# Two stacked graph-attention layers on one core: another written order, score tiles of 32x64, bias rows on VectorE, b2 in norm 1's shift, norm 3 on ScalarE

## The chip, the cores and the metric

The kernel runs on one core of one Trainium2 chip. The metric is the device time of that core in microseconds; three runs of the kernel before gave 3072.71, 3078.34 and 3072.94, so the median is 3072.94. Each profile is one further execution. An engine's records in it are written PE (TensorE's matmuls), PEld (its weight loads), DVE (VectorE), ACT (ScalarE), POOL (GpSimd) and SP (SyncE, which here only issues DMAs).

## The reference

32 independent graphs of 512 nodes with 256 features in f32, and an integer adjacency matrix of 512x512 for each. Two layers, both with a residual and a final layer norm; all norms are over the 256 features. Attention has 8 heads of 32.

```python
# layer 0, with allowed = (adj > 0) | (adj.T > 0) | eye
q, k, v = split(x @ Wqkv.T + bqkv)                      # per head
attn = softmax(where(allowed, (q / sqrt(32)) @ k.T, -inf)) @ v
x1 = layernorm(x + attn @ Wo.T + bo) * g1 + be1          # norm 1
y = relu(x1 @ W1.T + b1) @ W2.T + b2                     # hidden size 1024
z = layernorm(x1 + y) * g2 + be2                         # norm 2
x2 = layernorm(x + z)                                    # norm 3
# layer 1, with the mask adj != 0
q, k, v = x2 @ Wq.T + bq, x2 @ Wk.T + bk, x2 @ Wv.T + bv
attn = softmax(where(adj != 0, q @ k.T / sqrt(32), -inf)) @ v
out = layernorm(x2 + attn @ Wo.T + bo)                   # norm 4
```

## The kernel before

**Tiling.** A graph's 512 nodes are NQ = 4 blocks of 128; its 256 features are ND = 2 blocks of 128, each with HPC = 4 heads. Scores are computed transposed, with keys on partitions: score step k (0 to 7) is four heads of one feature block against one block of 128 keys, so p[k] is a tile of 128 x (4 heads x 512 queries). Per layer there are eight such steps. Each is: `scores` (four matmuls psS into four PSUM banks, L342, and Exp on ScalarE, L346), `masked` (a multiplication by the 0/1 mask on VectorE, L351), `product` (four matmuls psA = v.T p, accumulated over the four key blocks, L359; after the fourth, a copy to cT on ScalarE, L369). Row sums of p come from tiles of p that are first added up, partly by accumulating DMAs on GpSimd's queue (`pair`, L374), partly on VectorE (`fold`, L378), and then multiplied by a matrix of ones (`sums`, psR, L399). `divide` (L411 to L418) transposes the sums in blocks of 32, inverts, transposes back and scales cT; two small GpSimd adds (L414, L415) collect a guard against overflow, which selects a slow general path after the main program when it trips (it doesn't here).

**Dense parts.** `query_key` (psQK), `value` (psV), `project` (psO), `hidden` (psH) and `mlp` (psF) all go through `dense` (L171): with `wide=True` one matmul of 128x128 weights, otherwise four of 128x32, one for each quarter of the output partitions. `transpose` (psT, L308) turns x1 and x2 by matmuls with the identity, always 128x128. psS uses tiles of 32x128: contraction over the 32 features of a head, 128 keys. The tensors are f32 throughout, and an f32 matmul stands in the trace as two records.

**Norms.** y = PSUM + residual (L446), bn_stats and bn_aggr (L427, L428), 1/sqrt(var + eps) on GpSimd in two instructions (`root`, L433 and L434), then for norms 1 and 2 two VectorE instructions (L441, L442) with g and b, for norm 3 one VectorE instruction (`norm3`, L507), for norm 4 a small VectorE instruction (`offset`, L516: -mean/std) and an ACTIVATE with scale and bias on ScalarE (`norm4`, L521).

**Bias rows.** bov[layer] = bv Wo + bo is computed once (`value_bias`, L163, L166). Four accumulating DMAs per graph on GpSimd's queue (`add_row`, L174) add rows to a whole 128 x (4 x 256) tile: bov[0] to x1 (which starts as a second load of x), be2 to x, b2 to x1 after `transpose`, and bov[1] to x2.

**Input.** `cast` (L209) has GpSimd's queue turn adj into bf16 in HBM; `entries` loads it straight and, by four DMA transposes, transposed, and `masks` (L227 to L231) makes the two masks from them. x reaches its transposed form xT without TensorE: a DMA transpose of 16-bit halves (`flip`, L266), four small DMAs that sort the halves (`sort`, L283), and two ScalarE copies (`join`, L296); only graph 0 uses `transpose`.

**Order.** Nothing is scheduled automatically. The calls stand one under another by hand in `opening`, `period` and `closing`, inside `tc.manual_schedule()`, and each engine and each DMA queue runs its instructions strictly in that order, waiting where data or a buffer is not there. A period holds 70 groups of TensorE work, one graph's worth, but from several graphs (a, b, c, d, e, oldest first) at different stages: here layer 1's end of a, layer 0's end and layer 1 of b, layer 0 of c, the input of d and e. Buffers that set a limit: one psS tile (four banks, so the next scores wait for the Exp before), one accumulator psA, three banks of tag "d" for all other PSUM results, eight p tiles.

Of the kernel before, what the change touches and what calls it, by code (L numbers as in the profile page):

```python
# [18 lines left out]
EPS = 1e-5  # L19
# [8 lines left out]
def kernel(ctx: ExitStack, tc: tile.TileContext, t: dict, out: bass.AP):  # L28
# [88 lines left out]
    bo.append(spread("L1_gnn_bo"))  # L117

# [31 lines left out]
    def plain(pools: ExitStack):  # L150
# [6 lines left out]
        BEATS = ND * NQ  # L157
# [9 lines left out]

        def dense(out, lhsT, rhs, start, stop, wide):

            for at in (slice(0, P),) if wide else [slice(j * HD, (j + 1) * HD) for j in range(HPC)]:  # L170
                nc.tensor.matmul(out[at], lhsT[:, at], rhs, start=start, stop=stop)  # L171

        def add_row(dst, row):
            nc.gpsimd.dma_start(out=dst, in_=row[:, None, :].to_broadcast([P, NQ, D]), accum_op=ALU.add)  # L174

        class Absent:


            def __getattr__(self, name):
                return lambda *args, **kw: None  # L180

        class Graph:


            def __init__(self, b):
                self.b = b
                self.mv, self.rs, self.pf, self.total = {}, {}, {}, {}

            def tile(self, tag, shape, dtype=F32, **kw):
                t = work.tile([P, *shape], dtype, tag=tag, name=f"{tag}_{self.b}", **kw)  # L190
                setattr(self, tag, t)
                return t


            def load(self):
                if not hasattr(self, "x"):
                    nc.sync.dma_start(out=self.tile("x", [NQ, D]), in_=x[self.b].rearrange("(c p) d -> p c d", p=P))

            def again(self):

                if not hasattr(self, "x1"):
                    nc.sync.dma_start(out=self.tile("x1", [NQ, D]), in_=x[self.b].rearrange("(c p) d -> p c d", p=P))

            def cast(self):

                if hasattr(self, "code"):
                    return
                self.code = hbm.tile([N, N], BF16, tag="code", name=f"code_{self.b}")
                nc.gpsimd.dma_start(  # L209
                    out=self.code.rearrange("(p c) k -> p (c k)", p=P),  # L210
                    in_=adj[self.b].rearrange("(p c) k -> p (c k)", p=P),
                )

            def entries(self):

                if hasattr(self, "m0"):
                    return
                nc.sync.dma_start(
                    out=self.tile("m0", [NQ, N], BF16), in_=self.code.rearrange("(c p) k -> p c k", p=P)
                )  # L220
                self.tile("m1", [NQ, N], BF16, bufs=3)
                for i in range(NQ):
                    nc.sync.dma_start_transpose(out=self.m1[:, i, :], in_=self.code[:, i * P : (i + 1) * P])

            def masks(self):

                nc.vector.tensor_tensor(self.m0, self.m0, self.m1, ALU.max)  # L227
                diagonal = self.m0.rearrange("p c (k q) -> p (c k) q", q=P)[:, :: NQ + 1, :]
                nc.vector.tensor_tensor(diagonal, diagonal, ident_b[:, None, :].to_broadcast([P, NQ, P]), ALU.max)
                nc.vector.tensor_scalar(self.m0, self.m0, 0.0, None, ALU.is_gt)  # L230
                nc.vector.tensor_scalar(self.m1, self.m1, 0.0, None, ALU.not_equal)  # L231
# [6 lines left out]
            def once(self):  # L238

                if self.b == 0:  # L240
                    value_bias(0)

            def once1(self):
                if self.b == 0:
                    value_bias(1)

            def residual(self):

                add_row(self.x1, bov[0])
                add_row(self.x, be2)  # L250

            def flip(self, n, i):


                if i == 0:
                    self.tile("v", [NQ, D])
                    self.tile("kT", [ND, N])
                if n > 0:  # L260
                    h, j = divmod(i, 2)
                    dst, src = self.flipped(n, h)[:, :, j * P : (j + 1) * P], getattr(self, f"x{n}")[:, i, :]
                    nc.sync.dma_start_transpose(out=dst, in_=src.bitcast(U16))
                elif self.b > 0:
                    src = x[self.b, i * 2 * P : (i + 1) * 2 * P, :]
                    nc.sync.dma_start_transpose(out=self.flipped(0, i), in_=src.bitcast(U16))  # L266

            def flipped(self, n, h):
                t = self.x2[:, :2, :] if n == 1 else self.v[:, 2 * h : 2 * h + 2, :]
                return t.rearrange("p c d -> p (c d)").bitcast(U16).rearrange("p (a q) -> p a q", q=2 * P)  # L270

            def sorted(self, n, h):
                t = self.x2[:, 2:, :].rearrange("p c d -> p (c d)") if n == 1 else self.kT[:, h, :]
                return t.bitcast(U16).rearrange("p (a q) -> p a q", q=2 * P)

            def sort(self, n, h):

                if n == 0 and self.b == 0:
                    return
                src, dst = self.flipped(n, h), self.sorted(n, h)  # L280
                for w in range(2):
                    for i in range(2):
                        nc.sync.dma_start(  # L283
                            out=dst[i * P // 2 : (i + 1) * P // 2, w * ND : (w + 1) * ND, :], in_=src[w::2, i::2, :]
                        )

            def join(self, n, h):
                if n == 0 and self.b == 0:

                    self.transpose(self.x, h)  # L290
                    return
                if h == 0:
                    self.tile("xT", [ND, N])
                words = self.xT.bitcast(U16).rearrange("p c (q w) -> p c q w", w=2)
                for w in range(2):
                    nc.scalar.copy(  # L296
                        words[:, :, h * 2 * P : (h + 1) * 2 * P, w], self.sorted(n, h)[:, w * ND : (w + 1) * ND, :]
                    )


            def transpose(self, src, h):

                if h == 0:
                    self.tile("xT", [ND, N])
                ps = ps_d.tile([P, ND, 2 * P], F32, tag="d", name=f"psT_{self.b}_{h}")
# [5 lines left out]
                nc.scalar.copy(self.xT[:, :, h * 2 * P : (h + 1) * 2 * P], ps)  # L311

            def value(self, layer, h, wide=False):
                if h == 0 and layer != 0:
                    self.tile("v", [NQ, D])
                ps = ps_d.tile([P, 2, D], F32, tag="d", name=f"psV_{self.b}_{h}")
                for j in range(2):
                    at = slice((2 * h + j) * P, (2 * h + j + 1) * P)
                    for i in range(ND):
                        dense(ps[:, j, :], self.xT[:, i, at], proj[layer][0][2][:, i, :], i == 0, i == ND - 1, wide)  # L320
                nc.scalar.copy(self.v[:, 2 * h : 2 * h + 2, :], ps)

            def query_key(self, layer, which, c, h=None, wide=False):

                tag = ("qT", "kT")[which]
                dst = getattr(self, tag) if c or h or (which and layer == 0) else self.tile(tag, [ND, N])
                w, bias = proj[layer][0][which], proj[layer][1 + which]
                at = slice(0, N) if h is None else slice(h * 2 * P, (h + 1) * 2 * P)
                ps = ps_d.tile([P, at.stop - at.start], F32, tag="d", name=f"psQK_{self.b}_{which}_{c}_{h}")
                for i in range(ND):  # L330
                    dense(ps, w[:, i, c * P : (c + 1) * P], self.xT[:, i, at], i == 0, i == ND - 1, wide)
# [3 lines left out]
            def scores(self, layer, k):  # L335
                if k == 0:
                    self.layer, self.p, self.acc = layer, {}, {}
                hg, kc = divmod(k, NQ)
                s = ps_s.tile([P, HPC, N], F32, tag="s", name=f"psS_{self.b}_{k}")
                for j in range(HPC):  # L340
                    at = slice(j * HD, (j + 1) * HD)
                    nc.tensor.matmul(  # L342
                        s[:, j, :], self.kT[at, hg, kc * P : (kc + 1) * P], self.qT[at, hg, :], start=True, stop=True
                    )
                p = work.tile([P, HPC, N], F32, tag="p", name=f"p_{self.b}_{k}", bufs=8)
                nc.scalar.activation(p, s, AF.Exp, scale=SCALE)  # L346
                self.p[k] = p

            def masked(self, layer, k):
                p, m = self.p[k], (self.m0, self.m1)[layer]  # L350
                nc.vector.tensor_tensor(p, p, m[:, k % NQ, None, :].to_broadcast([P, HPC, N]), ALU.mult)  # L351

            def product(self, k):
                hg, kc = divmod(k, NQ)
                if kc == 0:
                    self.acc[hg] = ps_a.tile([P, N], F32, tag="acc", name=f"psA_{self.b}_{hg}")
                for j in range(HPC):
                    h = hg * HPC + j
                    nc.tensor.matmul(  # L359
                        self.acc[hg][j * HD : (j + 1) * HD, :],  # L360
                        self.v[:, kc, h * HD : (h + 1) * HD],
# [1044 lines left out]
```

## Time and profile before

| | |
|---|---|
| median of three runs | 3072.94 us |
| the profiled execution | 3073.78 us |
| its span, first to last instruction | 3072.0 us |
| mean granted TensorE clock | 0.999 |
| VectorE: mask multiplications L351 | 512 of 2278 ns, 1155.1 us |
| VectorE: folds L378 | 189 of 2286 ns, 429.4 us |
| ScalarE: Exp L346 | 512 of 1881 ns, 963.0 us |
| GpSimd: issue of `add_row`'s DMAs L174 | 128, in three rows 87.7, 58.9 and 41.8 us |
| TensorE: psS L342 | 4096 records, 583.9 us |
| DMA | 408.46 MB, mean 133 GB/s |

Busy times of TensorE are unions of records whose ends are modelled, and records of neighbouring groups overlap; the starts are what is measured. A row of groups gives line, engine, operation, output<-inputs, shape, count, busy us and mean ns of one, then the idle time of the engine before them and what ended it. A row of waits reads: engine and line that waited, engine and line that released it, us in total, times, the longest.

### The profile page before, as it was taken

To read this page: it belongs to the slowest core of one execution; us is meant where nothing else is said; L and a number is where in the kernel's file an instruction comes from. 1 tells how busy PE (TensorE), PEld (TensorE's weight loads), DVE (VectorE), ACT (ScalarE), POOL (GpSimd) and SP (SyncE) were. 2 spreads that over 40 slices of the span, in tenths; PEclk is the share of its full clock that TensorE was granted. 3 is DMA by queue.
4 is the path that set the end of the run, shared out by engine and by line. 5 is a ranking of instruction groups with operands and counts; after the bars stand their busy time and mean duration, and the time that the engine had idled before them with its cause. 6 is when DMAs were issued, how large, how long until landed. Compare 5 with 4: busy or idle time off the path is not lost.

```text
span 3072.0 us, 74202 instructions
## 1 busy us (share of the span) xinstructions
PE 3030.7 (99%) x32110; PEld 1434.9 (47%) x32110; DVE 2648.1 (86%) x3458; ACT 1708.2 (56%) x1983; POOL 1054.4 (34%) x1254
## 2 busy tenths in 40 slices
PE   8999999999999999999999999999999999999998
PEld 3544444444444444444444444544445444444453
DVE  6798889888889888898888988889888889888887
ACT  5455555555556555565555655565555556555554
POOL 1333233333334332343323333333433334332332
PEclk9999999999999999999999999999999999999999
DMA  9876667766777666676666866667766767666543
GB/s 196 167 133 138 116 140 147 142 124 122 139 141 144 122 131 128 138 153 124 134 122 135 154 133 133 115 141 145 141 125 126 136 138 147 128 126 125 117 84 70
DMA packets 341182, 408.46 MB, mean 133 GB/s; under 512 B 149617, under 2 KB 315633, under 8 KB 316145
## 3 DMA queue, kind: packets, MB, share of 16 engines
q0 software_dynamic: 95824, 282.09, 51.1%
q1 hardware_dynamic: 245024, 121.56, 16.3%
q8 instruction: 254, 4.16, 0.5%
q14 instruction: 80, 0.65, 0.1%
HBM read 89.01 MB, written 33.55 MB: 40 GB/s over the span
## 4 chain that ended last, share of the span: by engine, by line
PE 71%; DVE 19%; DMA 3%; issue 3%; POOL 2%; SPq 0%; ACT 0%; POOLq 0%; DVEq 0%; ACTq 0%
PE psH L171 13%; PE psF L171 13%; PE psS L342 11%; PE psA L359 9%; PE psQK_None L171 9%; DVE p L351 7%; PE psV L171 5%; PE psO L171 3%; PE psR L399 3%; PE psQK L171 2%; DVE p L378 2%; PE psT L308 2%; DMA p<-p 2%; DVE st L427 2%; DVE rT L417 1%
## 5 line engine op out<-in xcount | busy, mean ns | idle before, releaser
L346 ACT ACTIVATE p<-psS 128x2048 f32<-128x2048 f32 x512 | 963.0, 1881 | 641.0 <-PE psS L342 640.4
L351 DVE TENSOR_TENSOR p<-p,m 128x2048 f32<-128x2048 f32 x512 | 1155.1, 2278 | 9.0 <-ACT p L346 8.9
L433 POOL TENSOR_SCALAR rs<-mv 128x2 f32<-128x2 f32 (+1 forms) x320 | 333.8, 1043 | 939.6 <-DVE mv L428 937.2
L342 PE MATMUL psS<-qT,kT 32*128 32x512 f32 x4096 | 583.9, 640 | 3.2 <-ACT p L346 1.3
L359 PE MATMUL psA<-p,v 128*32 128x512 f32 x4096 | 493.4, 598 | 1.3 <-ACT cT L369 0.7
L171 PE MATMUL psF<-w_L_gnn_W,hT 128*32 128x256 f32 (+1 forms) x5024 | 464.1, 380 | 0.0
L171 PE MATMUL psH<-xT,w_L_gnn_W 128*32 128x256 f32 x8072 | 461.7, 380 | 1.6 <-DMA w_L_gnn_W<-in_L_gnn_W_dram 1.6
L378 DVE TENSOR_TENSOR p<-p,p 128x2048 f32<-128x2048 f32 x189 | 429.4, 2286 | 7.4 <-DMA p<-p 6.2
L171 PEld LDWEIGHTS psF<-w_L_gnn_W,hT 128*32 128x32 f32 (+1 forms) x5024 | 326.0, 127 | 168.1 <-issue 69.2
L171 PEld LDWEIGHTS psH<-xT,w_L_gnn_W 128*32 128x32 f32 x8072 | 260.1, 110 | 229.1 <-issue 48.3
L434 POOL TENSOR_TENSOR rs<-rs,neg_half 128x2 f32<-128x2 f32 (+1 forms) x320 | 300.6, 940 | 26.9
L342 PEld LDWEIGHTS psS<-qT,kT 32*128 32x128 f32 x4096 | 159.9, 182 | 318.9 <-issue 130.6
L480 ACT ACTIVATE hT<-psH,c_L_gnn_b 128x256 f32<-128x256 f32 x512 | 215.0, 472 | 118.6 <-PE psH L171 117.2
L414 POOL TENSOR_TENSOR total<-total,sT 128x16 f32<-128x16 f32 x128 | 28.7, 224 | 733.3 <-DVE sT L411 733.3
L359 PEld LDWEIGHTS psA<-p,v 128*32 128x32 f32 x4096 | 111.5, 109 | 314.1 <-issue 237.9
L171 PE MATMUL psQK_None<-xT,w_L_gnn_Wqkv 128*128 128x512 f32 (+1 forms) x608 | 238.9, 598 | 2.6 <-DMA w_L_gnn_Wqkv<-in_L_gnn_Wqkv_dram 2.6
L171 PE MATMUL psO<-w_L_gnn_Wo,cT 128*32 128x256 f32 (+1 forms) x3352 | 239.9, 380 | 1.1 <-DVE cT L418 1.0
L369 ACT COPY cT<-psA 128x512 f32<-128x512 f32 x128 | 75.1, 586 | 282.1 <-PE psA L359 282.1
L446 DVE TENSOR_TENSOR y<-psF,x 128x256 f32<-128x256 f32 x128 | 53.8, 420 | 198.5 <-PE psF L171 196.0
L374 POOL DMA_DIRECT2D p<-p x189 | 188.3, 996 | 102.0 <-PE psA L359 92.1
L171 PEld LDWEIGHTS psO<-w_L_gnn_Wo,cT 128*32 128x32 f32 (+1 forms) x3352 | 141.8, 116 | 95.0 <-DVE cT L418 21.0
L427 DVE BATCH_NORM_STATS2 st<-y 128x6 f32<-128x256 f32 x384 | 164.4, 428 | 13.1
(68 smaller groups left out, 2862.8 us busy)
## 6 DMA issues: line engine op xcount, KB each, us to landing
p<-p POOLq DMA_DIRECT2D x189, 1024.0 KB, 8.3
x<-in_x_dram SPq DMA_DIRECT2D x64, 512.0 KB, 5.6
x<-bov POOLq DMA_DIRECT2D x64, 512.0 KB, 9.6
code<-in_adj_dram POOLq DMA_DIRECT2D x32, 512.0 KB, 8.0
m<-code SPq DMA_DIRECT2D x32, 512.0 KB, 4.9
x<-s_L_gnn_ln_b POOLq DMA_DIRECT2D x32, 512.0 KB, 10.9
x<-s_L_gnn_b POOLq DMA_DIRECT2D x32, 512.0 KB, 5.4
out_dram<-x SPq DMA_DIRECT2D x32, 512.0 KB, 6.8
```

The source lines that it names most:

```text
L171: nc.tensor.matmul(out[at], lhsT[:, at], rhs, start=start, stop=stop)
L342: nc.tensor.matmul(s[:, j, :], self.kT[at, hg, kc * P : (kc + 1) * P], self.qT[at, hg, :], start=True, stop=True)
L346: nc.scalar.activation(p, s, AF.Exp, scale=SCALE)
L351: nc.vector.tensor_tensor(p, p, m[:, k % NQ, None, :].to_broadcast([P, HPC, N]), ALU.mult)
L359: nc.tensor.matmul(self.acc[hg][j * HD : (j + 1) * HD, :], self.v[:, kc, h * HD : (h + 1) * HD], self.p[k][:, j, :], start=(kc == 0), stop ...
L374: nc.gpsimd.dma_start(out=self.p[k], in_=self.p[k + 1], accum_op=ALU.add)
L378: nc.vector.tensor_tensor(self.p[dst], self.p[a], self.p[b], ALU.add)
L399: nc.tensor.matmul(self.total[hg][j * HD : (j + 1) * HD, :], ones, self.p[i][:, j, :], start=first and i == beats[0], stop=last and i == b ...
L427: nc.vector.bn_stats(st, y)
L433: nc.gpsimd.tensor_scalar(rs, self.mv[n][:, a:b, 1:2], EPS, None, ALU.add)
L434: nc.gpsimd.tensor_tensor(rs, rs, neg_half[:, a:b, None], ALU.pow)
L480: nc.scalar.activation(self.hT[h][:, f + j, :], ps[:, j, :], AF.Relu, bias=b1[:, f + j : f + j + 1])
```

## The change

The computation is the same; both masks, the softmax and its guard stay. The changes are:

- `scores` issues eight matmuls with tiles of 32x64 (half of the keys each) for four of 32x128, into the same PSUM tile.
- `add_row` and its DMAs are gone, and so is the second load of x (`again`). `bias` makes VectorE write x1 = x + bov[0], x = x + be2 and x2 = x2 + bov[1].
- b2 is no longer added to x1. Norm 1's shift be1 takes it, once, and since the hidden layer sees that shifted x1 too, W1.b2 is subtracted from b1, once (`hidden_bias`).
- `norm3` is gone; norm 3 uses `offset` and `norm` as norm 4 does, on ScalarE.
- Methods are cut into single instructions or groups (`scores` and `exp`, `add`, `stats`, `aggregate`, `center`, `affine`, each `relu`, each `sort` and `entry`), and opening, period and closing are written anew: TensorE's groups per period are again 70, in another sequence; the opening starts five graphs and the closing ends five.

The core of the diff:

```diff
+        def hidden_bias():
+            ps = ps_d.tile([P, NF], F32, tag="d", name="psB_2")
+            for f in range(NF):
+                for c in range(ND):
+                    nc.tensor.matmul(
+                        ps[:, f : f + 1],
+                        w1[:, c, f * P : (f + 1) * P],
+                        b2_c[:, c : c + 1],
...
+            nc.vector.tensor_tensor(b1, b1, ps, ALU.subtract)
+            nc.vector.tensor_tensor(be1, be1, b2, ALU.add)
...
-        def add_row(dst, row):
-            nc.gpsimd.dma_start(out=dst, in_=row[:, None, :].to_broadcast([P, NQ, D]), accum_op=ALU.add)
...
+            def bias(self, i):
+                row = (be2, *bov)[i][:, None, :].to_broadcast([P, NQ, D])
+                dst = self.x if i == 0 else self.x1 if i == 1 else self.x2
+                nc.vector.tensor_tensor(dst, self.x2 if i == 2 else self.x, row, ALU.add)
...
-                    nc.tensor.matmul(
-                        s[:, j, :], self.kT[at, hg, kc * P : (kc + 1) * P], self.qT[at, hg, :], start=True, stop=True
-                    )
+                    for half in range(2):
+                        key = kc * P + half * P // 2
+                        nc.tensor.matmul(
+                            s[half * P // 2 : (half + 1) * P // 2, j, :],
+                            self.kT(layer)[at, hg, key : key + P // 2],
+                            self.qT(layer)[at, hg, :],
...
-            def norm3(self, i):
-                mean, rs = self.mean(3, i), self.rs[3][:, i, :]
-                nc.vector.tensor_scalar(self.x2[:, i, :], self.y.pop(i), mean, rs, ALU.subtract, ALU.mult)
...
+            def norm(self, n, i):
+                nc.scalar.activation(
+                    self.x2[:, i, :], self.y(n, i), AF.Identity, bias=self.ms(n)[:, i, :], scale=self.rs(n)[:, i, :]
+                )
```

TensorE's order in one period, before and after (S scores, A product, R sums, T transpose, V value, Q query_key, O project, H hidden, F mlp; a w marks wide=True, and T is always wide):

```
before  S H H S H H S F R A S A F O S T Ow S A A A S T Qw A S Q Q Q Q S A A A R S Q R S V V
        S O O S A A A S T Vw S H H H H S T Qw Vw Qw Qw Fw Qw Fw A R A A A
after   Qw Vw T A Q Q S Q A A S R Q A V S A R Q S Q Q O V S A V S T Ow S H A H S A H H S A Q
        S F A A A R S T Fw S H H R S H A A H S A F A S F S T Ow Ow Qw
```

Three places of the new order that the prediction speaks of. The head of a period, where layer 0 of b ends (norms 2 and 3 of row block 2, transpose of x2):

```
a.add(4, 0)
a.stats(4, 0)
b.root(2, 2, 3)
b.affine(2, 2)
b.root(3, 3, 4)
b.offset(3, 3, 4)
a.add(4, 1)
c.context(0, 0)
a.add(4, 3)
b.stats(3, 2)
b.aggregate(3, 2)
b.query_key(1, 0, 0, 0, wide=True)
b.root(3, 2, 3)
d.entries()
a.add(4, 2)
b.norm(3, 3)
b.offset(3, 2, 3)
b.norm(3, 2)
...
b.value(1, 0, wide=True)
b.transpose(2, 1)
c.product(0, 4)
```

The end of a period, just ahead of that (c there is b here):

```
d.exp(0, 7)
d.masked(0, 4)
c.mlp(2)
c.add(2, 2)
c.stats(2, 2)
c.center(2, 3)
d.scores(0, 6)
c.norm(3, 1)
c.root(2, 3, 4)
c.affine(2, 3)
c.norm(3, 0)
c.transpose(2, 0)
b.guard(1, 0, 1)
d.exp(0, 6)
b.project(1, 0, wide=True)
c.stats(3, 3)
c.aggregate(3, 3)
b.project(1, 1, wide=True)
c.transpose_out(2, 0)
c.query_key(1, 1, 0, 0, wide=True)
c.query_key_out(1, 1, 0, 0)
c.aggregate(2, 2)
c.center(2, 2)
```

TensorE's groups at the start of the opening (before: `T T Qw Qw Vw S Q S V S Q S A ...`) and at the very end of the closing (before: `... S A R A S V R S Q S Q V S O S A R S O S A A A A A R A A O O`):

```
opening  T T Qw Qw S Q S Q S V S V S S A A A S A Q Q S ...
closing  ... S V S Q S Q S V S A A S A A S A S A R R A A O O
```

## Prediction

> **What bounds the kernel now.** I read the page's engine lines first, then busy time by stretches, then TensorE's timeline of one stretch, then the waits.
>
> The page's header:
>
> ```profile
> span 3072.0 us, 74202 instructions
> ...
> PE 3030.7 (99%) x32110; PEld 1434.9 (47%) x32110; DVE 2648.1 (86%) x3458; ACT 1708.2 (56%) x1983; POOL 1054.4 (34%) x1254
> ```
>
> TensorE (PE) has no slack; VectorE (DVE) is the next engine. Busy time in two stretches of one period each:
>
> ```profile
> 1000.00:1094.74 94.74, 94.26 (x1008) 44.62 (x1004) 82.83 (x109) 53.30 (x62) 33.52 (x39) 1.00 0.68 134
> 2000.00:2094.74 94.74, 94.27 (x1008) 44.63 (x1004) 82.82 (x109) 53.32 (x62) 33.49 (x40) 1.00 0.69 133
> ```
>
> Columns: stretch, its length, busy PE, PEld, DVE, ACT, POOL, clock, DMA share, GB/s. The second row is the first again: the kernel repeats itself exactly, 94.74 us per graph (the stores are 94.73 apart). So the question is what one period of TensorE costs. Its timeline (start, us, group):
>
> ```profile
> 1503.66 1.14 PE L342 MATMUL psS<-qT,kT 32*128 32x512 f32 x8
> 1504.73 3.66 PE L171 MATMUL psF<-w_L_gnn_W,hT 128*32 128x256 f32 x64
> 1508.44 1.07 PE L399 MATMUL psR<-p,ones 128*32 128x512 f32 x8
> 1509.29 1.07 PE L359 MATMUL psA<-p,v 128*32 128x512 f32 x8
> 1510.29 1.14 PE L342 MATMUL psS<-qT,kT 32*128 32x512 f32 x8
> 1511.36 1.07 PE L359 MATMUL psA<-p,v 128*32 128x512 f32 x8
> ```
>
> Look at starts, not durations: psR to psA takes 0.85-0.86, psS to whatever follows 1.07, though both move four tiles of 512 columns twice. The single starts behind these lines say why. An f32 matmul is two passes. Four tiles start 7 ns apart; a pass of 512 columns takes 0.429, one of 256 takes 0.216, narrow (128x32 tiles) as wide (128x128). Only a change of tile form costs more: the last narrow pass before another form is 0.113 longer (0.093 wide, 0.109 psS), and the first pass in a new form is longer by 0.104 (psS, loads of 128 columns) or 0.024 (narrow, 32 columns); two transposes pay 0.115 together. psS thus is 0.858 + 0.104 + 0.109 = 1.07.
>
> One graph: 16 psS, 16 psA and 4 psR at 0.858; 4 transpose groups at 0.436; psV, psO, psH 4+4+8 at 1.728; psQK 13.75; psF 4 at 3.456: 87.86. Form changes per period, counted in the written order (S scores, N narrow, W wide): NS 14, SN 12, SW 4, WS 2, WN 2. Leaving: 14x0.113 + 16x0.108 + 4x0.093 = 3.68. Entering: 16x0.104 + 14x0.024 + 4x0.115 = 2.46. Sum 94.00; the measured 94.74 leaves **0.74 of waits**. What they are, from the waits:
>
> ```profile
> PE psT L308 <- DVE x L442: 14.0, 30, 0.7
> ```
>
> and a smaller one of psR after psF (6.1 us in all). 32 x 94.74 = 3031.7, so 40 us are start and end.
>
> **What the skill says.** "TensorEngine Tiling (Array Packing)", Key Properties: a change of tiling mode drains TensorE, and tiles load and multiply in parallel. The trace agrees: 0.093-0.113 at every change, none between different matmuls in one form. "TensorE: Matmul & The Clock Gate", LDWEIGHTS: a load lasts its columns / 1.2 ns, whatever the rows: estimates 107 for 128 columns, 53 for 64, 27 for 32. The trace's 104 and 24 agree, and that identifies the first-pass excess as a load that nothing covers. The same page, Part 3, has concurrent tiles start some 4 ns apart; here it is 6.7, which I use.
>
> **The change, part by part.** Times against the profiled execution: span 3072.0, its own time 3073.78; the median of the runs, 3072.94, is 0.9 above the span.
>
> *Scores as eight 32x64 tiles.* Work is unchanged if all eight run side by side. First load: 64 columns, 0.051 on the line through 24 and 104 (bounds: 0.024, and 0.104 if the halves load in turn). Leaving: psS drains 0.109 - 3x0.0067 = 0.089 after its last tile starts; eight tiles start over 7x0.0067 = 0.047, so 0.135 (bounds: 0, if no drain is needed between two column-tiled forms, and 0.135). New psS: 0.858 + 0.051 + 0.135 = 1.044, against 1.071: -0.027 x 512 = **-13.6**.
>
> *Order: form changes.* New period: NS 14, SN 13, SW 3, WS 2, WN 1. One wide block less: 0.115 + 0.093 - 0.024 = 0.18. Over the kernel 102 wide blocks, not 128: 26 x 0.19 = **-4.9**.
>
> *Order: waits on TensorE.* Transpose (1,0): after project(0,0) come psV, psA, psV and two psS, 6.6 us, before it; norm 1's chain is two adds, stats and aggregates 2.0, root 0.8 on POOL (two short rows seen, 0.22 + 0.57), two centers and affines 1.9: about 5. That 0.44 wait goes. Transpose (2,0) now waits for ScalarE's norm(3,1) and norm(3,0), behind exp(0,7): ScalarE is free at the start of scores (0,6), needs 2x0.60 and a handover, scores take 1.04: about 0.3 late. Transpose (2,1) I take as just covered (rival 3). Net -0.14 x 30 = **-4** (bounds -22, all waits gone, and +30).
>
> *Bias rows on VectorE, norm 3 on ScalarE.* Three adds of 128x1024 f32, not seen before: half of fold L378's 2.29, 1.15 (1.22 with the fixed part whole): +3.45. Three offsets for norm 3 at 0.153: +0.46. Gone: L507, 4x0.405 = 1.62. VectorE 82.8 to **85.1** per period of 93.4 (91%, was 87%). ScalarE +4x0.60: 53.3 to 55.7. On TensorE's path this costs 0 while VectorE is covered; if the cover were gone, 2.3 per period, 74 us. Norm 3 as an ACTIVATE adds a wait for the offset on VectorE; queued behind it on ScalarE are the next exp and relu, and for x2 wait the transposes. POOL loses L174's three rows (87.7 + 58.9 + 41.8 = 188 us, 5.9 per period); root, pairs and guards queue behind less. DMA loses 128 adds and 32 loads of 512 KB, 84 of 408 MB; pairs (8.3 us to land) meet less traffic. Neither is on the path: taken as 0.
>
> *SP and POOL queues.* SP's entries, transposes and sorts go singly, in another order; they feed the next graph's join and masks a good part of a period ahead (a sort lands in 4.0 us, an entry in 2.7): 0.
>
> *b2.* norm 1's shift takes b2, so b1 gets W1.b2 once: 32 passes of one column in 128-column loads, between 32x0.026 (the two one-column matmuls of ps_total are that far apart) and 32x0.107: I take the upper with two form changes, **+3.7**, in the opening.
>
> *Opening and closing.* Six scores, 3.14 apart at least (17.58, 20.72, 23.86 in the timeline: one PSUM buffer, emptied by a 1.88 exp), now stand before the first product, with two psQK and two psV between, 13.2 us of work in some 16.8; before it was 15.9 in 17.7: +1.8. The last eight scores have fillers of 1.7 where 2.1 are needed: +1.5. The rest of both is a new order that I can't price. I take **+2** (bounds -6 and +10).
>
> Sum: -13.6 - 4.9 - 4 + 3.7 + 2 = -16.8: span 3055.2, as a median **3056**.
>
> **Rivals.**
> 1. *No drain between 32x64 and 128x32*, both column-tiled. Saves per period 13x(0.135 + 0.024) + 14x(0.113 + 0.051) = 4.4, 140 us: 2916. Against it: wide and narrow, of equal rows, drain in full, and so does psS. 0.07.
> 2. *The order also takes the remaining waits*, another 20 us: 3036. For it: they are two places only. 0.17.
> 3. *VectorE becomes late (slower).* Place: head of a period, transpose (2,1). From psF's end add, stats, center, affine, stats, aggregate and offset of row block 2, with those of block 3 and the a.add(4,.) between, are 6.4 on VectorE, two roots 1.5 with handovers, norm 0.6: 8.5 to 9.5, and a root next to a masked of 2.28 takes up to 2.7 on POOL (L433 shows 2.69). TensorE's cover: psS, two transposes, two psO, two psQK, psV and changes, 9.1. It costs nothing up to 9.1 and decides from 0.7 per period over that (3079); at 1.0: 3088. For it: VectorE at 91%. Against: in this stretch its instructions are short. 0.18.
> 4. *The halves load in turn*, so the first load stays 0.104 while eight starts lengthen the drain: psS 1.097, +0.027 instead of -0.027: 3056 + 27 = 3083. Against it: narrow tiles' four loads start 7 ns apart and cost 24, not 4x27. 0.13.
> The forecast, within 11 us either way: 0.45.
>
> **How the numbers follow.** This kernel's measurement tells 0.2%, 6 us, from no change: 3067 to 3079 is "same". Faster: 0.40 of the forecast, all of 1 and 2: 0.64. Same: 0.05 of the forecast, 0.06 of rival 3, 0.04 of 4: 0.15. Slower: 0.21. The range goes from the unknown order's good end below rival 2 (3030) to rival 3 at 1.0 (3088); outside are rival 1 and the tail of 3.
>
> **What would show it.** psS as 32*64, 8192 records, the next group 1.04-1.05 after its start: right; 1.10: rival 4; 0.86: rival 1. Stores 93.4 to 94.1 apart: right; 94.7 or more, with TensorE waiting at psT for ACT x2 or DVE: rival 3. DVE about 85 per period, POOL under 28, no L174. I am wrong if psS keeps 1.07 or more, or if a wait of TensorE that is not in the list above exceeds 0.7 per period.

## The result and the profile after

| | before | after |
|---|---|---|
| median | 3074.11 us (4 runs, 3072.71 to 3078.34) | **3046.22 us** (4 runs, 3045.4 to 3049.06) |
| ratio, 95% interval | | 0.9909 [0.9891, 0.9926] |
| profiled execution, span | 3073.78, 3072.0 us | 3046.83, 3044.7 us |
| stores of the steady part, apart (mean of 16) | 94.79 us | 93.22 us |
| DMA | 408.46 MB | 325.32 MB |

The forecast was 3056, the sum of its terms -16.8; the span fell by 27.3. The page's header after:

```profile
span 3044.7 us, 85990 instructions
...
PE 3006.8 (99%) x38410; PEld 1359.9 (45%) x38410; DVE 2667.0 (88%) x3524; ACT 1736.5 (57%) x2111; POOL 947.7 (31%) x1126
```

Busy time in one period (length, busy PE, PEld, DVE, ACT, POOL, clock, DMA share, GB/s):

```profile
1000.00:1093.21 93.21, 93.21 (x1200) 42.23 (x1192) 83.45 (x111) 54.22 (x67) 31.31 (x35) 1.00 0.53 109
```

PE is busy for the whole stretch: 93.21 of 93.21, where it was 94.26 of 94.74. VectorE is busy for hardly longer (82.83 before). TensorE's timeline:

```profile
1003.62 1.11 PE L399 MATMUL s<-qT,kT 32*64 32x512 f32 x16
1004.67 1.07 PE L419 MATMUL acc<-p,v 128*32 128x512 f32 x8
1005.55 3.64 PE L186 MATMUL psH<-xT,w_L_gnn_W 128*32 128x256 f32 x64
1009.12 1.11 PE L399 MATMUL s<-qT,kT 32*64 32x512 f32 x16
1010.16 1.06 PE L419 MATMUL acc<-p,v 128*32 128x512 f32 x8
```

psS (s in these lines, and psA is acc) is 1.04 to 1.05 from its start to the next group's: 1003.62 to 1004.67, 1009.12 to 1010.16. Inside, its first pass is 0.051 longer than 0.429, and its last one 0.135.

**Where the time went.** For each pair of neighbouring passes I took the distance of their starts, less the 0.429, 0.216 or 0.109 of the pass, and summed it by kind of step over 16 steady periods. The passes themselves are 87.86 per graph in both kernels.

| us per period | before | after | x 32 | predicted |
|---|---|---|---|---|
| psS, first load | 1.67 | 0.82 | | |
| psS, leaving it | 1.75 | 2.17 | | |
| *both: 32x64 tiles* | | | **-14.0** | -13.6 |
| leaving wide blocks | 0.37 | 0.28 | **-3.0** | -4.9 |
| inside transposes, psT waits included | 0.91 | 0.18 | | |
| inside narrow groups, psR waits included | 0.62 | 0.32 | | |
| entering psS | 1.61 | 1.59 | | |
| *these three: waits* | | | **-33.5** | -4 |
| start and end: span less 32 periods | 38.6 | 61.7 | **+23.1** | +5.7 |

"Waits included" means that these rows also hold the cost of the form itself. After the change nothing else is in them: in the changed kernel TensorE waits for nothing between 300 and 2480 us.

Sum: -27.4. Two terms were about right and two far off, in opposite directions. The experiments are about these two, and about why the new order can hide what it hides.

### The profile page after: what moved, and what is told of

It reads as the page before. It is cut to its first block, busy times and chain, and to the rows that moved or that the text cites. A ratio compares the mean times of both kernels' runs of the same rounds, so it can differ in the third digit from the quotient of the medians.

```text
span 3044.7 us, 85990 instructions
## 1 busy us (share of the span) xinstructions
PE 3006.8 (99%) x38410; PEld 1359.9 (45%) x38410; DVE 2667.0 (88%) x3524; ACT 1736.5 (57%) x2111; POOL 947.7 (31%) x1126
## 2 busy tenths in 40 slices
DMA packets 257017, 325.32 MB, mean 107 GB/s; under 512 B 147329, under 2 KB 231425, under 8 KB 231937
## 4 chain that ended last, share of the span: by engine, by line
PE 97%; ACT 1%; DMA 1%; DVE 0%; issue 0%; POOL 0%; SPq 0%; DVEq 0%; ACTq 0%
PE s L399 18%; PE acc L419 15%; PE psH L186 15%; PE psF L186 15%; PE psQK_None L186 11%; PE psO L186 7%; PE psV L186 7%; PE psR L443 4%; PE psQK L186 4%; PE psT L360 2%; ACT p L408 1%; DMA p<-p 0%; DMA w_L_gnn_Wqkv<-in_L_gnn_Wqkv_dram 0%; PE psB L173 0%; DVE p L435 0%
## 5 line engine op out<-in xcount | busy, mean ns | idle before, releaser
L408 ACT ACTIVATE p<-s 128x2048 f32<-128x2048 f32 x512 | 962.9, 1881 | 558.7 <-PE s L399 484.6
L399 PE MATMUL s<-qT,kT 32*64 32x512 f32 x8192 | 571.2, 613 | 4.9 <-ACT p L408 4.0
L419 PE MATMUL acc<-p,v 128*32 128x512 f32 x4096 | 513.7, 597 | 1.3 <-DVE p L412 1.3
L186 PE MATMUL psH<-xT,w_L_gnn_W 128*32 128x256 f32 (+1 forms) x8024 | 480.4, 380 | 0.7 <-ACT xT L365 0.7
L186 PE MATMUL psF<-w_L_gnn_W,hT 128*32 128x256 f32 x6704 | 466.2, 380 | 0.0
L467 POOL TENSOR_TENSOR total<-total,sT 128x16 f32<-128x16 f32 x128 | 191.8, 1498 | 703.6 <-DVE mv L499 399.7
L186 PEld LDWEIGHTS psH<-xT,w_L_gnn_W 128*32 128x32 f32 (+1 forms) x8024 | 262.3, 111 | 268.6 <-issue 46.2
L186 PEld LDWEIGHTS psF<-w_L_gnn_W,hT 128*32 128x32 f32 x6704 | 287.3, 116 | 197.5 <-issue 36.4
L399 PEld LDWEIGHTS s<-qT,kT 32*64 32x64 f32 x8192 | 119.3, 130 | 310.7 <-issue 143.7
L186 PE MATMUL psQK_None<-xT,w_L_gnn_Wqkv 128*32 128x512 f32 (+1 forms) x1988 | 241.0, 595 | 4.7 <-DMA w_L_gnn_Wqkv<-in_L_gnn_Wqkv_dram 4.7
L186 PEld LDWEIGHTS psO<-w_L_gnn_Wo,cT 128*32 128x32 f32 (+1 forms) x2056 | 168.8, 136 | 65.7 <-issue 12.9
```

Of the source, the lines that this page charges most:

```text
L399: nc.tensor.matmul(s[half * P // 2 : (half + 1) * P // 2, j, :], self.kT(layer)[at, hg, key : key + P // 2], self.qT(layer)[at, hg, :], st ...
L408: nc.scalar.activation(self.p(layer, k), self.at("s", (layer, k), [HPC, N]), AF.Exp, scale=SCALE)
L419: nc.tensor.matmul(acc[j * HD : (j + 1) * HD, :], self.v(layer)[:, kc, h * HD : (h + 1) * HD], self.p(layer, k)[:, j, :], start=(kc == 0), ...
L467: nc.gpsimd.tensor_tensor(total, total, src, ALU.add)
```

## The experiments

All times are medians; the ratio is to the kernel before, on the same chip. "Apart" is the distance of two stores in the steady part, in most of the periods. Differences to the changed kernel are of medians that were taken on several chips. The kernel before had medians of 3072.9 to 3074.1 on them, so a difference of about 1 us says nothing.

**1. Tiles alone, in the new order and in the old one.** The first kernel puts 32x128 back into the changed kernel:

```diff
-                    for half in range(2):
-                        key = kc * P + half * P // 2
...
+                    nc.tensor.matmul(
+                        s[:, j, :],
+                        self.kT(layer)[at, hg, kc * P : (kc + 1) * P],
+                        self.qT(layer)[at, hg, :],
...
```

> The changed kernel with score tiles of 32x128 again, its order and the rest kept. Theory (the last pass of a score group and the next group's first pass decide): psS back to 1.07 from its start to the next group's, 0.027 more in each of 512 groups: +13.6 us over the changed kernel, stores 93.64 apart instead of 93.21. Rival (what the tiles save is mostly given back in waits, since ScalarE and VectorE get 13.6 us less time for their work): the time rises by under 5 us, and TensorE's waits shrink.

3060.62 (3058.17 to 3061.48), 0.9957 [0.9943, 0.9970]: +14.4 on the changed kernel, stores 93.63 apart, no wait in the steady part. The theory held. The second makes the opposite edit, and no other, in the kernel before:

> The kernel before with score tiles of 32x64 and nothing else. Theory: -13.6 us against the kernel before (0.4%), psS 1.044, stores 94.31 apart, the waits of psT for VectorE unchanged at 0.65 per period. Rival (a group that ends sooner only makes the transposes wait longer, since VectorE has not become faster): between 0 and -5 us, with the wait of psT for VectorE grown toward 0.75.

3075.62 (3071.23 to 3080.37), 1.0004 [0.9995, 1.0012]: **nothing gained**. The rival held, and went further than I had set it. psS has the same 0.051 and 0.135 as in the changed kernel, but most periods are only 0.08 shorter (94.66) and some are longer. TensorE's waits, before and then in this kernel (us in total, times, longest):

```profile
PE psT L308 <- DVE x L442: 14.0, 30, 0.7
```

```profile
PE psT L308 <- DVE x L448: 21.2, 32, 0.7
PE psR L405 <- DVE p L384: 5.5, 5, 2.4
```

The wait of psT has grown from 14.0 to 21.2, and psR's from 1.4 (`PE psR L399`) to 5.5. Most of what TensorE saved on the scores, 0.44 per period, it spent waiting for a norm and a fold of VectorE: the wait at psT alone is 0.28 longer in a usual period.

**2. The order of one group.** In the kernel before, psV moved ahead of the transposes that wait:

```diff
+            d.value(0, 0, wide=True)
             c.transpose(c.x1, 0)
...
-            d.value(0, 0, wide=True)
```

> The kernel before with one group moved: psV of the next graph's first columns stands ahead of the transposes of row block 0 that wait for VectorE, instead of behind them. It tells what the new order's gain in waits is worth by itself. Theory (the waits are a matter of order and are worth their full length): the 0.65 per period of psT for VectorE goes, about 30 times: -19 us against the kernel before, less what two more or fewer changes of tile form cost (none by count). Rival (the wait comes back one step further on, since what VectorE delivers late is needed by the chain behind it as well): under 5 us, with a new wait of psH, psR or psA in its place.

3053.48 (3052.54 to 3059.4), 0.9939 [0.9925, 0.9952]: -19.8, stores 94.12 apart, no wait of psT for VectorE left. The theory held. One line of the order was worth more than the tiles. With the tiles added to it:

> The kernel before with both: psV of the next graph's first columns ahead of the transposes that waited, and score tiles of 32x64. The tiles alone gave nothing there (0.08 off the period), the move alone 0.62 off the period and about 20 us. Theory (the tiles' gain was eaten by the wait of psT for VectorE, and the move takes that wait away): the tiles now give 0.43 per period over the move alone, stores 93.69 apart, about -13.6 us against the move alone, near 3040. Rival (VectorE or the loop through it as a whole paces the old order, the next wait takes the gain): stores 93.9 to 94.1 apart, at most -5 us against the move alone, with psR or psA waiting.

3047.18 (3046.8 to 3049.04), 0.9917 [0.9904, 0.9931]: -6.3 on the move alone, between the two expectations. Most periods are 93.78, 0.34 of the 0.43 hoped for; in the rest the next wait has come up:

```profile
PE psR L405 <- DVE p L384: 6.2, 6, 2.4
```

So the same edit is worth 0, 6.3 or 14.4, and what decides is how much cover the order leaves: in the first two cases the profile shows longer waits of TensorE for VectorE, in the third it shows none.

**3. Norm 3 and the bias rows: what the new order needs from them.** In the changed kernel, norm 3 as one VectorE instruction again, in the places where `norm` stood:

```diff
+                if n == 3:
+                    nc.vector.tensor_scalar(
+                        self.x2[:, i, :], self.y(3, i), self.mv(3)[:, i, 0:1], self.rs(3)[:, i, :], ALU.subtract, ALU.mult
+                    )
+                    return
```

(`offset` does nothing for norm 3.)

> The changed kernel with norm 3 as one VectorE instruction of 0.41 each again, in place of an offset on VectorE and a 0.60 pass on ScalarE: VectorE +1.2 per period, to 85.4 of 93.2; ScalarE -2.4. Theory (VectorE has cover to spare in this order): within 3 us of the changed kernel, stores 93.2 apart. Rival (the order has just enough cover, and VectorE late at the second transposes is next): stores more than 93.5 apart with a wait of psT, +10 us or more.

3093.28 (3092.76 to 3097.95), 1.0066 [1.0052, 1.0080]: **+47 on the changed kernel**, stores 94.85 apart. My theory fell. The rival had the size, and the wait is at psT:

```profile
PE psT L360 <- DVE x L527: 46.0, 30, 1.8
```

But the rival named VectorE's load and the second transposes, and this wait is at the first ones. The timeline of the changed kernel there (start, us, engine, line, output<-inputs, idle before):

```profile
1045.45 1.88 ACT L408 ACTIVATE p<-s 128x2048 f32<-128x2048 f32 x1 [4.10 <-PE s L399]
1047.22 1.08 ACT L525 ACTIVATE x<-z,ms,rs 128x256 f32<-128x256 f32 x2
...
1049.00 0.42 DVE L493 TENSOR_TENSOR y<-psF,x 128x256 f32<-128x256 f32 x1 [1.58 <-PE psF L186]
...
1049.90 0.66 PE L360 MATMUL psT<-ident,x 128*128 128x128 f32 x4
```

and of the kernel with norm 3 on VectorE:

```profile
1060.84 2.26 DVE L412 TENSOR_TENSOR p<-p,m 128x2048 f32<-128x2048 f32 x1
...
1064.67 0.42 DVE L493 TENSOR_TENSOR y<-psF,x 128x256 f32<-128x256 f32 x1 [1.58 <-PE psF L186]
...
1065.86 0.41 DVE L527 TENSOR_SCALAR x<-z,mv,rs 128x256 f32<-128x256 f32 x1
...
1066.78 0.41 DVE L527 TENSOR_SCALAR x<-z,mv,rs 128x256 f32<-128x256 f32 x1
...
1067.24 0.66 PE L360 MATMUL psT<-ident,x 128*128 128x128 f32 x4 [1.59 <-DVE x L527]
```

On ScalarE both norms end at 1048.30, 1.6 ahead of psT. On VectorE they stand behind an add that has to wait 1.58 until psF ends, though their own inputs were there 4 us before that add starts. VectorE has time (it stood idle for that 1.58); the norms have the wrong place in its queue. To tell place from load, only their place was changed, in the repeated part:

```diff
-            c.offset(3, 0, 2)
+            c.norm(3, 1)
+            c.norm(3, 0)
             d.exp(0, 4)
...
             d.masked(0, 4)
             c.mlp(2)
             c.add(2, 2)
...
-            c.norm(3, 1)
...
-            c.norm(3, 0)
```

> The kernel with norm 3 on VectorE, which lost 47 us to a wait of 1.6 per period at the first transposes of norm 3's result, with one thing moved in the repeated part: the two norms of row blocks 1 and 0 stand on VectorE where the offset stood, ahead of the mask product of 2.26 and of the add that waits 1.58 for psF, instead of behind that add. The work of every engine is the same. Theory (what was lost is the place in VectorE's queue, behind an instruction that waits for TensorE, and not VectorE's time): the wait goes, stores 93.2 apart, within 6 us of the changed kernel. Rival (VectorE's 1.2 more per period are too much for this order): stores more than 93.8 apart, the wait moved to psF, acc or the second transposes.

3053.51 (3053.03 to 3054.68), 0.9935 [0.9921, 0.9948]; stores **93.19** apart, with VectorE busier than in the changed kernel:

```profile
1000.00:1093.21 93.21, 93.21 (x1194) 42.39 (x1193) 84.47 (x112) 52.22 (x63) 30.74 (x35) 1.00 0.52 109
```

The theory held for the repeated part: place, not load. The time lies 7.3 above the changed kernel, not within 6. Opening and closing keep the bad place, and their gaps on TensorE are some 7 to 8 longer (27.8 and 15.4, against 25.2 and 10.2).

The bias rows, by DMA again in the changed kernel (x1 by a second load of x):

```diff
-                nc.vector.tensor_tensor(dst, self.x2 if i == 2 else self.x, row, ALU.add)
+                nc.gpsimd.dma_start(out=dst, in_=row, accum_op=ALU.add)
```

> The changed kernel with its three bias rows added by accumulating DMAs from the POOL queue again (x1 by a second load of the input), the order kept. Theory (VectorE is covered at 84 of 93 us and the DMA engines are not on the path either): within 3 us of the changed kernel, stores 93.2 apart, VectorE 80.6 per period, POOL's guards and rows up. Rival (VectorE's 3.7 per period were what the order had to hide): no gain in the steady stretch, as no wait is left there. Rival 2 (rows queued on POOL ahead of roots and pairs): waits of psT or psR return, +10 us or more.

3056.98 (3053.17 to 3064.0), 0.9953 [0.9941, 0.9965]: +10.8. The stores still average 93.2 apart, so the VectorE time that the rows take is indeed covered. But the time is not within 3 of the changed kernel's: that part of the theory fell. Rival 2 had the size, not the place. The profiled execution is the fastest of the six, 6.7 above that of the changed kernel, and there the loss is in single events. The one in the steady part is at psO's residual, for which a row comes late, and not at psT or psR:

```profile
308.83 0.42 DVE L494 TENSOR_TENSOR y<-psO,x 128x256 f32<-128x256 f32 x1 [3.94 <-DMA x<-bov]
...
310.65 1.60 PE L186 MATMUL psQK<-xT,w_L_gnn_Wk 128*128 128x256 f32 x4 [3.69 <-DVE y L494]
```

Besides, the first psQK starts at 13.3 instead of 11.9, the closing has 3.9 more of gaps, and the end is 1.3 shorter. What made the other executions up to 11 longer is in no trace.

**4. The opening.** In the changed kernel the opening shows:

```profile
11.94 2.90 PE L186 MATMUL psQK_None<-xT,w_L_gnn_Wqkv 128*128 128x512 f32 x3 [4.73 <-DMA w_L_gnn_Wqkv<-in_L_gnn_Wqkv_dram]
...
69.50 3.63 PE L173 MATMUL psB<-c_L_gnn_b,w_L_gnn_W 128*128 128x1 f32 x32
...
73.16 0.17 DVE L180 TENSOR_TENSOR c_L_gnn_b<-c_L_gnn_b,psB 128x8 f32<-128x8 f32 x1 [4.30 <-PE psB L173]
...
77.67 1.09 PE L360 MATMUL psT<-ident,x 128*128 128x128 f32 x4 [3.50 <-DVE x L522]
...
79.42 9.87 PE L186 MATMUL psH<-xT,w_L_gnn_W 128*128 128x256 f32 x32 [0.67 <-ACT xT L365]
```

Wqkv lands 2.6 later than before (9.37). psB's 32 passes take 3.56 until the next group; VectorE stops 4.30 at the subtraction, with norm 1 behind it, and psT then waits 3.50. psH after that takes 9.87 where 32 passes of 0.216 are 6.9, because TensorE runs at half clock there (shown in the last section). First, the step left out (`a.once(2)` removed, so that b2 is missing from the output):

> The changed kernel without the once-only step that takes W1.b2 from b1 (left out: that subtraction and the sum of norm 1's shift and b2, so b2 is missing from the output). Theory (the step costs its passes and the stall behind them, since VectorE takes its instructions in order and waits at the subtraction): -8 to -11.5 us against the changed kernel. Rival (as predicted: its passes alone): -3.7.

3040.02 (3038.37 to 3040.63), 0.9889 [0.9875, 0.9903]: **-6.2**. Between the two: the passes are 3.5 of it, and psT still waits 2.15 for VectorE, with psH as slow. The stall is only partly the step's doing; I had charged all of it.

Then the step moved ahead of `a.fold(0, 2, 2, 0)`, its weights loaded earlier:

> The changed kernel with the once-only step for b2 moved ahead of the last fold of the opening, and the loads of its weights issued earlier. Theory (a stall of VectorE at a bad place): the 3.50 wait of the transposes for VectorE and part of the slow psH behind it go, the passes stay: about -8 us against the changed kernel. Rival (the opening is bound by the loads that arrive from memory, and earlier weights push back the queries and keys): between -2 and +5.

3045.0 (3043.42 to 3045.48), 0.9906 [0.9892, 0.9921]: -1.2, which is not clear of the noise. It is within the rival's range but not for its reason. The stall has moved:

```profile
56.70 0.16 DVE L180 TENSOR_TENSOR c_L_gnn_b<-c_L_gnn_b,psB 128x8 f32<-128x8 f32 x1 [7.24 <-PE psB L173]
...
57.12 4.49 DVE L435 TENSOR_TENSOR p<-p,p 128x2048 f32<-128x2048 f32 x2
59.55 1.08 PE L443 MATMUL psR<-p,ones 128*32 128x512 f32 x4 [2.88 <-DVE p L435]
```

VectorE stops 7.24 ahead of the folds, and psR waits for them. To this the order of the loads was added:

```diff
+            a.constants(4, 6)
+            a.constants(17, 20)
+            a.constants(10, 12)
             b.flip(0)
-            b.sort(0, 1, 0)
-            b.sort(0, 0, 0)
...
-            b.flip(1)
...
-            b.cast()
...
+            a.entry(3)
+            b.sort(0, 1, 0)
+            b.sort(0, 0, 0)
+            b.flip(1)
```

(excerpt; `cast` goes further down, behind `a.pair(0, 2)`)

> As the kernel with the early step for b2, and in addition the small constants first on the queue, and the flip, sorts and cast of the masks behind the weights of queries, keys and values. Theory (the opening lost 2.6 us because those weights land later than before: the first psQK starts at 11.9 instead of 9.4): another -2.5, about -10.5 against the changed kernel. Rival (the masks then arrive late for the first products): no gain over the kernel with the early step.

3041.63 (3041.36 to 3044.49), 0.9899 [0.9885, 0.9913]: another -3.4, the first psQK at 9.34. For this step the theory held, and this version is 4.6 below the changed kernel (span 3039.5 against 3044.7). Last, the passes and the subtraction of the step apart:

```diff
             a.once(0)
+            a.once(2)
...
             a.divide(0, 1)
+            a.once_out()
```

> As the kernel with the reordered opening, with the once-only step for b2 cut in two: its 32 passes stand on TensorE ahead of psO, where TensorE waits 1.9 for VectorE, and the subtraction stands on VectorE behind the product that psO waits for. Theory (moved early, the step only moved the stall, since VectorE stopped 7.2 at the subtraction ahead of the folds): the wait of psR of 3.1 shrinks below 1, -2 to -4 us against the reordered opening, about 3038. Rival (VectorE's chain through the masks and folds sets the opening whatever TensorE does): within 1 us of it.

3044.42 (3040.25 to 3044.86), 0.9902 [0.9887, 0.9918]. The time didn't follow the theory, though the place it named did: the first psR starts at 50.12 and not at 55.76, with 0.80 of wait. The wait of 3.2 is now at the second psR, and the fold ahead of that one waits for an accumulating DMA:

```profile
50.12 1.06 PE L450 MATMUL psR<-p,ones 128*32 128x512 f32 x8 [0.80 <-ACT kT L396]
...
56.61 2.29 DVE L442 TENSOR_TENSOR p<-p,p 128x2048 f32<-128x2048 f32 x1 [2.69 <-DMA p<-p]
...
59.05 1.94 PE L450 MATMUL psR<-p,ones 128*32 128x512 f32 x8 [3.24 <-DVE p L442]
...
68.29 5.37 PE L189 MATMUL psO<-w_L_gnn_Wo,cT 128*128 128x256 f32 x16
```

After it psO's 16 passes take 5.37, where 16 of 0.216 are 3.5. So VectorE's work doesn't set this place, as the rival had it: VectorE stands idle there, for a DMA. Whether this version is slower than the one before it stays open: the runs of the two overlap.

**5. Sixteen tiles.** A test of the arithmetic for psS, with 32x32 tiles in the changed kernel:

```diff
-                    for half in range(2):
+                    for part in range(4):
```

> The changed kernel with sixteen score tiles of 32x32 in place of eight of 32x64. Theory (first load by its columns, leaving by the number of tiles that start one after the other): first load 0.024, leaving 0.089 + 15 x 0.0067 = 0.189, sum 1.071: as slow as 32x128, +13.6 us over the changed kernel. Rival (only the columns of the first load count, the drain does not grow with the tiles): 0.024 + 0.135, 0.027 less per group: -14 us. Rival 2 (sixteen instructions cannot start at 6.7 ns within a pass): passes of over 0.429 themselves, more than +13.6.

3066.45 (3065.3 to 3069.75), 0.9979 [0.9972, 0.9986]: +20.2, stores 93.85 apart. In the commoner case the second pass starts 0.453 after the first (0.429 + 0.024) and the next group 0.618 after that (0.429 + 0.189): 1.071, as the theory had it. Some 38% of the groups take 1.087, with the last of the sixteen starts 0.016 late, and some wait as much at the entry; on average a group costs 0.040 more than with 32x64, not 0.027. The first rival, a drain that doesn't grow with the tiles, would have saved 14.

## Why the prediction came out as it did

**Scores in 32x64 tiles: right, as a term.** 0.051, 0.135 and 1.044 were predicted and measured, -14.0 against -13.6. Rival 1 (no drain) and rival 4 (halves in turn) are excluded by the same lines. But the sum assumed, without saying so, that work removed from TensorE counts in full. In the kernel before that is false: there these 13.6 were worth 0.

**Form changes: right in kind**, -3.0 against -4.9. The cost of a transpose group was read too high: it pays 0.055 to 0.059 where it waits for nothing in the kernel before, not 0.115.

**Waits on TensorE: the term that failed**, -33.5 instead of -4, or -1.05 instead of -0.14 per period. Three steps of it were wrong. First, what was there to gain: the 0.74 of waits was a remainder, and the transposes' 0.115 was too high by 4 x 0.06, so that some 0.23 of waits had been booked as form changes; 0.97 is close to the 1.05 that went. The wait of psT alone was not 0.44: moving psV took 0.62 off the period. Second, "ScalarE is free at the start of scores (0,6)" misread the order: between exp(0,7) and scores(0,6) stands `c.mlp(2)`, 3.6 on TensorE against an Exp of 1.88, so ScalarE was free 1.6 before psT and not 0.3 after. Third, the rest of the 0.74 was left standing, for no reason that the prediction gives. In a usual period of the kernel before it is mostly psR after psF, 0.22 late, and it went too. Rival 2, that the order takes the remaining waits, is what happened in the steady part.

**Bias rows, norm 3, queues: taken as 0.** For the bias rows that is shown for the steady part, with VectorE at 83.45 of 93.21. A row took the predicted 1.22, and VectorE's instruction times, added up, rose by 2.2 per period (86.8 to 89.0), as predicted. Its busy time, predicted as 85.1, rose by 0.6, because it counts only once the time in which neighbouring records overlap. Norm 3 on ScalarE was not a neutral part: at the place that the order gives it, it is worth 47 against the same place on VectorE (46 of it in the wait at psT). It isn't VectorE's time that counts, but that ScalarE's queue has nothing there that waits for psF. GpSimd's busy time came to 31.3 per period and not under 28: its first guard add takes 1.50 on average in this order, where it took 0.22 (192 us in all, against 29). No wait of TensorE in the steady part comes of it.

**Rival 3 (VectorE late at the second transposes)** didn't come, but "just covered" was right:

```profile
1056.62 0.60 ACT L525 ACTIVATE x<-z,ms,rs 128x256 f32<-128x256 f32 x1 [0.25 <-DVE ms L509]
...
1057.31 0.62 PE L360 MATMUL psT<-ident,x 128*128 128x128 f32 x4
```

The second norm ends at 1057.22, and psT starts 0.09 later, as soon as psV is through.

**hidden_bias: +6.2 instead of +3.7.** Its passes were right (3.56); that VectorE would stop at the subtraction was left out.

**Opening and closing: +17 instead of +2**, above the bound of +10. What I had priced was about right (the last scores, seven gaps of 0.23 over a change of form, are 1.6 against +1.5). What I called "a new order that I can't price" was the larger part. Against the kernel with psV moved, which has the old edges without the psT wait, TensorE's gaps over 0.15 (what a step between passes takes too long, passes at half clock included) are 12.9 longer in the opening (25.2 against 12.2). Up to the last psO they are 1.9 longer in the closing (5.8 against 3.9), and from the start of that psO's last pass to the end it is 2.5 longer (12.5 against 10.0). Of the opening's share the late Wqkv is 2.6 by its start, 3.4 by experiment, and 2.7 belong to the b2 step, which the kernel without it saves. Of the closing's, the products' 1.46 for a mask and psO's 1.16 are two single waits. At the end, the matmul that sums the overflow guard now stands behind the last norm, and the last store is issued behind it:

```profile
3036.09 0.58 ACT L525 ACTIVATE x<-y,ms,rs 128x256 f32<-128x256 f32 x1
...
3036.77 0.19 PE L2754 MATMUL ps_total<-ones,total_row 128*1 128x1 f32 x2 [4.22 <-ACT x L525]
...
3038.10 0.37 SPq L549 DMA_DIRECT2D out_dram<-x  x1
```

The store comes 1.43 after that norm; in the kernel with psV moved, where the guard's sum runs ahead of the last psO, it comes 0.02 after. No run moved the guard back, and the rest of both edges isn't traced one by one.

So the time came near the forecast because -29 of waits and +17 of edges were missed together. That is luck. The period, predicted as 93.4 to 94.1, was 93.2: outside.

## What to carry to other kernels

A saving on the busiest engine counts only where nothing else is about to be late; ask of each waiting place whether the saving lies ahead of it, and move work there before trimming. In engines that run in order, cost an instruction by what stands ahead of it in its queue and what that waits for, not by the engine's busy share: 0.8 us of norms lost 1.6 us per period behind one add, and nothing a few lines earlier. A hand-written order pays its opening and closing once: price these from their own timeline.

## What the runs showed of the hardware

- The first load of a tile form and its way out are separate costs. With score tiles of 128, 64 and 32 columns the first pass was 0.104, 0.051 and 0.024 longer; leaving cost 0.109, 0.135 and 0.189, which is 0.089 plus 0.0067 for each tile after the first. Of 32x128, 32x64 and 32x32, 32x64 is the cheapest here.
- TensorE at half clock after a wait shows as passes of 0.427 instead of 0.216. Stretches of the changed kernel, in the columns of above:

```profile
78.00:84.50 6.50, 5.83 (x16) 4.44 (x15) 5.32 (x12) 3.20 (x4) 2.31 (x4) 0.50 0.77 147
100.00:106.00 6.00, 6.00 (x116) 3.54 (x112) 3.84 (x12) 2.99 (x5) 1.60 (x4) 1.00 0.42 124
```

The Trainium skill, "TensorE: Matmul & The Clock Gate", Part 1, has the clock halved after an idle window of about 3.4 us. The 3.50 wait ahead of psT agrees. In the kernel without the b2 step the clock was halved after a wait of only 2.15, and in the one with the step early it was not after the same 2.15 (psT 0.63 instead of 1.08), so a wait's length alone does not decide.
